# Batch 1's statistics ahead of filters and matrices, raw matrices through two buffers, three buffers for the split's second terms

## The chip, the cores and the metric

The kernel runs on one core of a Trainium2 chip. The core has five engines that matter here: PE (TensorE, matmuls and transposes), DVE (VectorE), ACT (ScalarE), POOL (GpSimd) and SP (SyncE, which here only issues transfers). Each works through its own list of instructions, in the order in which they stand there, and waits on semaphores for the others. Data lies in HBM (DRAM), in SBUF (128 partitions) and, for PE's results, in PSUM. Transfers (DMAs) are issued by SP, ACT or POOL and carried out by 16 DMA engines.

The metric is the device time of one execution in microseconds (us). The kernel before took 2992.23 us, the median of three runs (2992.15, 2992.23, 2994.43).

## The reference, cut to what matters

Input is x of shape (2, 128, 64, 64): two batches of 128 channels and 4096 positions, here called tokens. Two layers follow each other.

```python
# layer 0: group norm, four attention heads of 32 channels with rotary positions, projection, residual
xn  = groupnorm(x) * gn_w + gn_b
q, k, v = split(w_qkv @ xn + b_qkv);  q, k = rotary(q), rotary(k)
a   = softmax(q.k) v                      # 4096 x 4096 scores per batch and head
x   = xn + w_proj @ a + b_proj
# layer 1: self-attention of the normalised tokens, then a spectral layer
t   = tokens(x)
y   = layernorm(t);   t = t + softmax(y y^T) y
u   = layernorm(t)
for i, frac in enumerate((1, 2, 4, 8)):   # four branches, sequences of 4096 / frac
    s_i = sum over 16 filters k of conv(phi_k, u) @ (sigma_k ** 0.25 * Mphi[i, k]) + short convolution with Mu[i]
t   = t + sum over i of weight_i * s_i    # weight: a straight-through argmax of four numbers
```

What is spoken of below: the values v of layer 0 and the stacks of its q and k; the statistics (mean and variance of each token) of layer 1's first layernorm; and the 16 pairs of 128 x 128 matrices M_phi_plus and M_phi_minus, of each of which the weighted sum over the four branches is needed.

## The kernel before

**Layer 0** (`layer0`, lines 175 to 451) runs four units: batch 0 and batch 1, in each two pairs of heads. A unit's q and k lie in SBUF as float16 stacks `qs` and `ks` (high and low parts of the numbers above each other), its values as three bfloat16 parts. `prepare` (L207) makes them. For i in 0..7 (512 tokens each), PE projects into a PSUM tile of tag "st" (two slots of three banks), `rotate` (L228) applies the rotary tables `tab` on DVE (two L236, a sum L240, high part L241, low part L242, largest value L243), and every second i `stacks` (L275) copies the terms by 16 DMAs into `qs` and `ks`. `split` (L264) takes the values out of PSUM into the tile `left` (L268) and cuts off three bfloat16 parts: a cast (L271), and a subtraction (L273) after the first two. `table(i + 2)` loads the table after next and is kept in program order on SP.

For the first unit all of this lies ahead of or between the first scores. There, and only there (`first`), the casts L271 and L241 go to ACT, the subtractions L273 to POOL, and the DMAs of the k stacks to SP, those of the q stacks to POOL. The later units are prepared beside the attention of the unit before, where `beside` is advanced by a step at certain groups. In attention, three blocks of scores are computed by PE (L190, into the same two slots of tag "st"), exponentiated by ACT (L433) and multiplied with v (L190). All of layer 0's matmuls are kept in program order.

**Layer 1's attention** is `attend` (L876), first for batch 0, then for batch 1. It walks over 36 pairs (j, i) with j <= i of 512 x 512 blocks: the scores are symmetric, so each block serves twice. Per pair: `scores` twice (L890 on PE, L899 on ACT), `turn` four times where i > j (transposes L906, ACT L908, DVE L909), `sums` of the pair before (DVE L947 and L948 four times each, products L916, DVE L954 or L956). At i = 7 `close(j)` finishes 512 tokens (L927 to L938).

Beside it runs a chain of helpers, given as `beside`. `attend` advances it by one step (from one `yield` to the next) after each of the two `scores`, and once inside and once after `sums`. For batch 0 the chain is built at L1083 and L1084:

```python
steps = normalise(1, p1, stage, gate)
attend(0, p1, chain(left, filters(p, fw), matrices(p), steps), closed, ready)
```

- `left`: what layer 0 still has to do, the last `divide` and `project`.
- `filters` (L792): phi through two small transforms into `tables` in DRAM, 5 steps; two tiles `tb` of tag "raw".
- `matrices` (L846): the branch weights, the weighted sum `mu`, then for each k of 16 a load of 512 KB in two DMAs into `raw` (L865, L866), a step, the weighted sum on DVE (L716 and three L718), sum and difference into the same tile (L871, L872), the store to `mx` in DRAM (L873), a step. The tag "raw" has one buffer.
- `normalise(1, ...)` (L742): first the statistics of batch 1's tokens, in eight steps of four tiles (bn_stats L690, aggregate L693, then L88 on DVE and the power L89 on POOL), then eight tiles i: normalised values y (L709), high part `hi`, transposes `yT` (L757), `hiT`, and the low parts. Tile i is held back by `gate` until `close(i)` has been done, because it overwrites what batch 0's attention reads.

`ready` (L1066) loads the low parts `low` for batch 0, eight loads of 512 KB into the one buffer of tag "low", in the pairs with j = 0.

**What sets the order.** A planner of the framework turns the program into a list for each engine. Among the instructions that its own clock holds to be ready, it takes the one that stands first in the program, so an instruction can be listed far from its place when others wait longer than the planner thinks or when its buffer comes free late. Tiles of one tag get their slots in program order. `tc.keep_in_program_order` ties an instruction behind the one that stands directly before it in the program on the same engine; the first bn_stats of every four and every L709 are tied so. On the chip the lists are fixed: an engine waits at the head of its list, whatever stands behind.

Of the kernel before, what the change touches and what calls it, by code (L numbers as in the profile page):

```python
# [12 lines left out]
F32 = mybir.dt.float32  # L13
# [9 lines left out]
P = 128  # L23
B, C, HH, WW = 2, 128, 64, 64
L = HH * WW
NH = 4
CH = C // NH
# [7 lines left out]
NK = 16  # L35
NU = 3
NBR = 4
# [26 lines left out]
def conv_attn_hybrid(ctx: ExitStack, tc: tile.TileContext, io):  # L64
    nc = tc.nc
# [32 lines left out]
    def chain(*parts):  # L98
        for p in parts:
            yield from p  # L100
# [74 lines left out]
    def layer0(tok, px, last, side, beside_last):  # L175
# [3 lines left out]
        with ExitStack() as l0:  # L179
            p1 = pool(l0, "l0_1")  # L180
            p2 = pool(l0, "l0_2", 2)
# [25 lines left out]
            def prepare(b, pr, xn):  # L207
# [3 lines left out]
                u = f"{b}_{pr}"  # L211
                qs = p2.tile([P, 2, L], F16, tag="qs", name=f"qs{u}")
                ks = p2.tile([P, 2, L], F16, tag="ks", name=f"ks{u}")
# [3 lines left out]
                first = (b, pr) == (0, 0)  # L217
# [46 lines left out]
                def split(at, n, pv):  # L264

                    bvb = bv[:, 2 * CH * pr : 2 * CH * pr + 2 * CH].rearrange("p (g c) -> p g c", g=2)
                    left = p2.tile([P, n, 2, CH], F32, tag="left", name=f"left{u}_{at}", bufs=1)
                    nc.vector.tensor_tensor(left, pv, bvb.unsqueeze(1).to_broadcast([P, n, 2, CH]), ALU.add)  # L268
                    for k in range(NV):
                        dst = v[:, at : at + n, :, CH * k : CH * k + CH]  # L270
                        (nc.scalar.copy if first else nc.vector.tensor_copy)(dst, left)  # L271
                        if k + 1 < NV:
                            (nc.gpsimd if first else nc.vector).tensor_tensor(left, left, dst, ALU.subtract)  # L273

                def stacks(i2, term):  # L275
                    for s, stack in enumerate((qs, ks)):
                        for g in range(2):
                            for r in range(4):
                                src = term[r // 2 if s else r % 2]
                                at = 64 * s + CH * g  # L280
                                (nc.sync if first and s else nc.gpsimd).dma_start(
                                    stack[CH * r : CH * r + CH, g, bass.ts(i2, 1024)],
                                    src[at : at + CH, :],
                                )
# [46 lines left out]
            ao = {}  # L331
# [40 lines left out]
            qs, ks, v, steps = prepare(0, 0, xn)  # L372
# [29 lines left out]
            for n, (b, pr) in enumerate(units):  # L402
# [12 lines left out]
                for g in range(2):  # L415
                    for i in range(NQ):
                        acc = psum.tile([P, 512], F32, tag="acc", name=f"acc{b}_{pr}_{g}_{i}", bufs=1)
                        for m, tiles in enumerate(groups):
# [12 lines left out]
                            e = p2.tile([P, GT, 512], F16, tag="e", name=f"e{b}_{pr}_{g}_{i}_{m}", bufs=3)  # L431
# [10 lines left out]
                if n + 1 < len(units):  # L442
                    for _ in beside:
                        pass
                    qs, ks, v, _ = after
# [278 lines left out]
    def layers(st, layer0):  # L724
# [3 lines left out]
        tok = [tokens[b].tile([P, NI, C], F32, tag="t", name=f"tok{b}") for b in range(B)]  # L728
        px = pool(st, "px", side="right")
        right0, right1 = (st.enter_context(ExitStack()) for _ in range(2))  # L730
        last = pool(right0, "last", 2, side="right")
# [7 lines left out]
            hiT.append(px.tile([P, L], F32R, tag="a", name="hiT"))  # L739
            hi.append(Columns([px.tile([P, HALF], F32R, tag=f"b{n}", name=f"hi{n}") for n in range(2)]))  # L740

        def normalise(b, p, stage, gate=None):  # L742

            stats = LayerStats(p, tok[b], f"a{b}")
            yield from stats.steps()
            for i in range(NQ):
                while gate is not None and gate[0] <= i:
                    yield
                cols = bass.ts(i, 512)
                y = stage(i, 0)  # L750
                for t in range(4):
                    stats.normed(y[:, bass.ts(t, P)], 4 * i + t)
                nc.vector.tensor_copy(hi[0][:, cols], y)
                yield
                pt = side[0](f"yT{b}_{i}")
                for t in range(4):
                    nc.tensor.transpose(pt[:, bass.ts(t, P)], y[:, bass.ts(t, P)], ident)  # L757
                nc.vector.tensor_copy(hiT[0][:, cols], pt)
                low = (stage(i, 1), stage(i, 0)) if b == 0 else (loT[0][:, cols], lo[0][:, cols])
                for n, (src, first) in enumerate(((pt, hiT[0][:, cols]), (y, hi[0][:, cols]))):  # L760
                    nc.vector.tensor_tensor(low[n], src, first, ALU.subtract)
                    if b == 0:
                        nc.sync.dma_start(lows[i, n], low[n])
                yield

        def beside_last(stage):
            first_parts()
            stages = [stage(n) for n in range(2)]
            yield from normalise(0, last, lambda i, n: stages[n][:, i])


        left = layer0(tok, px, last, side, beside_last)
# [73 lines left out]
        def matrices(p):  # L846
            wbr = branch_weights(p)
            mu_raw = p.tile([P, NBR, NU, C], F32, tag="raw", name="mu_raw")
            nc.scalar.dma_start(mu_raw, io["mu"].rearrange("i n d e -> d i n e"))
            weighted_sum(mu, mu_raw, wbr)  # L850
            nc.sync.dma_start(gw, io["gw"])
            nc.vector.tensor_tensor(gw, gw, mask.unsqueeze(1).to_broadcast([P, 2, P]), ALU.mult)

            sig = p.tile([P, NK], F32, name="sig")
            nc.gpsimd.dma_start(sig, io["sigma"].partition_broadcast(P))
            quarter = p.tile([P, NK], F32, name="quarter")
            nc.gpsimd.memset(quarter, 0.25)
            nc.gpsimd.tensor_tensor(sig, sig, quarter, ALU.pow)
            coef = p.tile([P, NK, NBR], F32, name="coef")
            for k in range(NK):  # L860
                nc.vector.tensor_scalar(coef[:, k, :], wbr, sig[:, k : k + 1], None, ALU.mult)
            yield
            for k in range(NK):
                raw = p.tile([P, NBR, 2, C], F32, tag="raw", name=f"raw{k}")
                nc.sync.dma_start(raw[:, :, 0, :], io["mpp"][:, k].rearrange("i d e -> d i e"))  # L865
                nc.sync.dma_start(raw[:, :, 1, :], io["mpm"][:, k].rearrange("i d e -> d i e"))  # L866
                yield
                pm = p.tile([P, 2, C], F32, tag="pm", name=f"pm{k}")
                weighted_sum(pm, raw, coef[:, k, :])
                own = raw[:, 0]  # L870
                nc.vector.tensor_tensor(own[:, 0, :], pm[:, 0, :], pm[:, 1, :], ALU.add)  # L871
                nc.vector.tensor_tensor(own[:, 1, :], pm[:, 0, :], pm[:, 1, :], ALU.subtract)  # L872
                nc.sync.dma_start(mx[k], own)  # L873
                yield

        def attend(b, p, beside, closed, ready=lambda i: None):  # L876
# [181 lines left out]
        with ExitStack() as l1:  # L1058
            p1 = pool(l1, "l1")
            lo.append(p1.tile([P, L], F32R, name="lo"))  # L1060
            fw = transform(p1)
            with ExitStack() as part:
                p = pool(part, "l1_a")
                gate = [0]

                def ready(i):  # L1066
                    for n in range(2) if i == 0 else [i + 1]:
                        if n < NQ:
                            low = p.tile([P, 2, 512], F32, tag="low", name=f"low{n}")
                            nc.sync.dma_start(low, lows[n].rearrange("n p c -> p n c"))  # L1070
                            nc.vector.tensor_copy(loT[0][:, bass.ts(n, 512)], low[:, 0])
                            nc.vector.tensor_copy(lo[0][:, bass.ts(n, 512)], low[:, 1])

                def closed(j):
                    gate[0] = j + 1

                y = [None]

                def stage(i, n):
                    y[0] = p.tile([P, 512], F32, tag="y", name=f"y1_{i}")  # L1080
                    return y[0]

                steps = normalise(1, p1, stage, gate)  # L1083
                attend(0, p1, chain(left, filters(p, fw), matrices(p), steps), closed, ready)  # L1084
            right0.close()

            mxr, mxl = (x[0].rearrange("p (k s c) -> p k s c", k=NK, s=2) for x in (hiT, loT))
            with ExitStack() as part:
                p = pool(part, "l1_b", 2)
                fed = LayerStats(ffw, tok[1], "f1")  # L1090

                def closed(j):
                    fed.take(range(4 * j, 4 * j + 4))
                    fed.close(range(4 * j, 4 * j + 4))
                    own = slice(2 * j, 2 * j + 2)
                    m = p.tile([P, 2, 2, C], F32, tag="m", name=f"m{j}")
                    nc.sync.dma_start(m, mx[own].rearrange("k p s c -> p k s c"))
                    nc.vector.tensor_copy(mxr[:, own], m)
                    nc.vector.tensor_tensor(mxl[:, own], m, mxr[:, own], ALU.subtract)

                attend(1, p1, feed(0, p, bank, fw), closed)
# [321 lines left out]
```

## Time and profile before

| | |
|---|---|
| profiled execution | 2991.11 us, span 2989.3 us, clock 0.983 |
| median of three runs | 2992.23 us |
| PE busy | 2862.9 us, 96% of the span |
| DVE, ACT, POOL busy | 1738.8, 1835.8, 665.1 us |
| layer 0 | to about 1030 us; its first unit is complete at about 74 us |
| layer 1's attention, batch 0 and batch 1 | about 1030 to 1450 and 1450 to 1830 us |
| spectral layer | about 1830 to 2989 us |

The span is the time from the first to the last instruction in the trace of one execution; the device time lies a little above it. "Busy" of an engine is the time in which it executes an instruction. In the row of 40 slices each digit is the busy share of a fortieth of the span, 74.7 us. In the tables of stretches each engine's busy time is followed by its number of instructions; the columns behind are PE's granted clock as a share of the full one, the mean share of time in which a DMA engine is busy, and GB/s. In the timelines a line is the start, the duration, the engine, the line of the kernel, the operation and its tiles; in brackets stands how long the engine was idle before and what released it. SPq is the issuing of a DMA by SP.

### The profile page before, as it was taken

Reading aid. Unit: us, or ns where it says so; the run is one execution under the profiler, and the core shown is the slowest. Engines: PE = TensorE matmul, PEld = TensorE weight load, DVE = VectorE, ACT = ScalarE, POOL = GpSimd, SP = SyncE. Lnnn points to the kernel's source line nnn. Section 1 sums busy time; section 2 is a strip of 40 time slices with the busy share of each in tenths; the row PEclk is TensorE's granted clock in tenths of the full one; section 3 lists DMA queues with packets and bytes.
Section 4 is the critical chain, followed back from the end, with each engine's and each line's share of the span. In section 5 each row is a group of like instructions: output and inputs, shape, how many; then the busy total and the mean of one; then the engine's idle time right before and its main releaser. Section 6 shows DMA issues by size and latency. Waiting matters only on the chain. (4 is left out here: it accounts for less than half of the span.)

```text
span 2989.3 us, 40111 instructions
## 1 busy us (share of the span) xinstructions
PE 2862.9 (96%) x13872; PEld 1822.1 (61%) x13872; DVE 1738.8 (58%) x3060; ACT 1835.8 (61%) x2363; POOL 665.1 (22%) x1328
## 2 busy tenths in 40 slices
PE   5999999999999999399999999999999999999997
PEld 2555555555455578288677786666666666666665
DVE  5364662364252389578866777555555555556553
ACT  4999999999999844144444454444444444444542
POOL 4031130021000000100101102433444444444440
PEclk9999999999999999699999999999999999999999
DMA  5021120021010132200011001333343334333331
GB/s 147 26 82 48 54 70 4 20 71 38 5 43 24 39 99 65 62 1 1 15 36 44 12 22 50 91 96 100 83 87 84 83 79 114 80 84 82 81 83 49
DMA packets 165777, 175.91 MB, mean 59 GB/s; under 512 B 45264, under 2 KB 109536, under 8 KB 165568
## 3 DMA queue, kind: packets, MB, share of 16 engines
q1 hardware_dynamic: 121760, 136.00, 16.4%
q0 software_dynamic: 40816, 34.04, 5.4%
q10 hardware_dynamic: 2992, 3.22, 0.3%
q8 instruction: 115, 1.88, 0.3%
q14 instruction: 94, 0.77, 0.1%
HBM read 130.68 MB, written 25.49 MB: 52 GB/s over the span
## 5 line engine op out<-in xcount | busy, mean ns | idle before, releaser
L433 ACT ACTIVATE e<-s 128x1536 f16<-128x1536 f32 (+1 forms) x704 | 936.7, 1428 | 35.9 <-PE s L190 31.0
L1174 DVE TENSOR_TENSOR xl<-cv,xh 128x1024 fp32r<-128x1024 f32 x512 | 603.0, 1219 | 436.5 <-ACT xh L1173 350.0
L1173 ACT CAST xh<-cv 128x1024 fp32r<-128x1024 f32 x512 | 494.7, 1018 | 523.6 <-PE cv L1164 511.8
L1139 POOL DMA_DIRECT2D tokens_in<-rows x1024 | 490.5, 487 | 680.5 <-PE cv L1164 577.1
L190 PE MATMUL s<-qs,ks 128*128 128x512 f16 x2048 | 557.5, 379 | 8.5 <-ACT e L433 3.4
L190 PE MATMUL acc<-e,v 128*97 128x512 f16 x2048 | 557.3, 379 | 3.4 <-DVE accs L389 0.2
L1196 PE MATMUL m<-xh,loT 128*128 128x512 f32 x1024 | 409.8, 400 | 0.0
L1196 PE MATMUL m<-xh,hiT 128*128 128x512 f32 x1024 | 403.2, 394 | 0.0
L190 PEld LDWEIGHTS <-v 128*97 128x97 bf16 x2048 | 254.6, 124 | 214.5 <-issue 12.5
L899 ACT ACTIVATE ey<-y,nshift 128x512 f32<-128x512 f32 x288 | 196.1, 690 | 302.1 <-PE y L890 214.8
L190 PEld LDWEIGHTS <-ks 128*128 128x128 f16 x2048 | 200.5, 99 | 227.6 <-issue 42.3
L1164 PE MATMUL cv<-tables_in,tokens_in 32*128 32x512 f32 x2048 | 300.0, 645 | 1.4 <-DVE xl L1174 1.2
L1196 PE MATMUL m<-xl,hiT 128*128 128x512 f32 x1024 | 292.3, 417 | 1.2 <-DVE xl L1174 0.5
L1196 PEld LDWEIGHTS m<-xl,hiT 128*128 128x128 f32 x1024 | 178.8, 189 | 175.8 <-issue 104.7
L1196 PEld LDWEIGHTS m<-xh,loT 128*128 128x128 f32 x1024 | 192.7, 188 | 90.7 <-issue 47.8
L1196 PEld LDWEIGHTS m<-xh,hiT 128*128 128x128 f32 x1024 | 192.4, 188 | 42.2
L916 PE MATMUL oacc<-ep,hi 128*128 128x512 f32 x576 | 209.4, 410 | 2.7 <-DVE ep L948 1.8
L909 DVE TENSOR_TENSOR eT<-eT,eT 128x512 fp32r<-128x512 f32 x224 | 146.0, 684 | 109.4 <-ACT eT L908 108.9
L389 DVE COPY accs<-acc 97x512 f32<-97x512 f32 x64 | 44.2, 690 | 275.2 <-PE acc L190 275.1
L948 DVE TENSOR_TENSOR ep<-ey,ep 128x512 fp32r<-128x512 f32 x288 | 191.9, 683 | 5.4 <-PE oacc L916 0.4
L908 ACT ACTIVATE eT<-eT 128x512 fp32r<-128x512 f32 x224 | 133.0, 607 | 94.6 <-PE eT L906 93.9
L916 PE MATMUL oacc<-eT,hi 128*128 128x512 f32 x448 | 155.7, 409 | 3.3 <-DVE oT L956 2.3
(191 smaller groups left out, 3024.0 us busy)
## 6 DMA issues: line engine op xcount, KB each, us to landing
tables_in<-tables SPq DMA_DIRECT2D x1024, 64.0 KB, 3.4
tab<-in_rot SPq DMA_DIRECT2D x32, 512.0 KB, 4.1
tokens_in<-rows POOLq DMA_DIRECT2D x1024, 16.0 KB, 3.2
qs<-term POOLq DMA_DIRECT2D x128, 64.0 KB, 2.2
rows<-uh SPq DMA_DIRECT2D x64, 128.0 KB, 1.9
ks<-term POOLq DMA_DIRECT2D x96, 64.0 KB, 1.9
accs<-back SPq DMA_DIRECT2D x32, 128.0 KB, 2.3
lows<-stage SPq DMA_DIRECT2D x16, 256.0 KB, 2.0
```

The lines of the kernel that those rows point to most:

```text
L190: tc.keep_in_program_order(nc.tensor.matmul(*args, **kw))
L433: nc.scalar.activation(e[:, own, :], ps[:, own, :], AF.Exp, scale=SCORE_SCALE)
L899: nc.scalar.activation(e[:, 2 * h + q, :], ps[:, q, :], AF.Exp, bias=nshift, accum_out=den[:, t, i : i + 1])
L908: nc.scalar.activation(eT[0], pt, AF.Copy, accum_out=den[:, 4 * i + u, j : j + 1])
L909: nc.vector.tensor_tensor(eT[1], pt, eT[0], ALU.subtract)
L916: nc.tensor.matmul(acc, a[0][:, own], c, start=(start and t == 0 and n == 0), stop=(stop and t == len(es) - 1 and n == 2),)
L948: nc.vector.tensor_tensor(es[t][1], e[:, t, :], es[t][0], ALU.subtract)
L1139: nc.gpsimd.dma_start(ut[part, :, :], rows[b][ci, row : row + BP, w0 : w0 + WC // 2, :])
L1164: nc.tensor.matmul(pu[:, h, :], ut[grp, w % 2, :], tt[grp, w % 2, :], start=True, stop=True)
L1173: nc.scalar.copy(hi, pu.rearrange("d h (c k) -> d k h c", k=NK))
L1174: nc.vector.tensor_tensor(seconds[n % 2][:, :, w, 64 * g2 : 64 * g2 + 64].rearrange("d k (h c) -> d k h c", h=2), pu.rearrange("d h (c k) ...
L1196: nc.tensor.matmul(acc, m, x, start=(s == 0 and w == 0 and i == 0), stop=(s == 1 and w == WC - 1 and i == len(products) - 1),)
```

## The change

Four things are changed.

1. In the first unit `left` takes one of three tiles in turn, of the tags "ao0" to "ao2", which hold layer 0's attention output later on. In the other units it keeps its own tag.
2. `stacks` issues the k stack before the q stack. In the first unit, half of the q stack's DMAs (r >= 2) goes to SP instead of POOL.
3. `normalise` gets its statistics handed in. For batch 1 they are computed right after `left`, before filters and matrices; the tiles follow after the matrices as before. For batch 0 the order stays.
4. `matrices` loads k = 0 and k = 1 ahead, then k + 2 one step after matrix k has been stored. Even k use the buffer of tag "raw", odd k that of tag "low", which is of the same size.

```diff
                 def split(at, n, pv):
-                    left = p2.tile([P, n, 2, CH], F32, tag="left", name=f"left{u}_{at}", bufs=1)
+                    pool_, tag = (p1, f"ao{at // n % 3}") if first else (p2, "left")
+                    left = pool_.tile([P, n, 2, CH], F32, tag=tag, name=f"left{u}_{at}", bufs=1)
...
                 def stacks(i2, term):
-                    for s, stack in enumerate((qs, ks)):
+                    for s, stack in ((1, ks), (0, qs)):
...
-                                (nc.sync if first and s else nc.gpsimd).dma_start(
+                                (nc.sync if first and (s or r >= 2) else nc.gpsimd).dma_start(
...
-        def normalise(b, p, stage, gate=None):
-            stats = LayerStats(p, tok[b], f"a{b}")
-            yield from stats.steps()
+        def normalise(b, stats, stage, gate=None):
             for i in range(NQ):
...
-            yield from normalise(0, last, lambda i, n: stages[n][:, i])
+            stats = LayerStats(last, tok[0], "a0")
+            yield from stats.steps()
+            yield from normalise(0, stats, lambda i, n: stages[n][:, i])
...
+            raws = {}
+            def load(k):
+                if k < NK:
+                    raws[k] = p.tile([P, NBR, 2, C], F32, tag="low" if k % 2 else "raw", name=f"raw{k}")
+                    nc.sync.dma_start(raws[k][:, :, 0, :], io["mpp"][:, k].rearrange("i d e -> d i e"))
+                    nc.sync.dma_start(raws[k][:, :, 1, :], io["mpm"][:, k].rearrange("i d e -> d i e"))
+            load(0)
+            load(1)
+            yield
             for k in range(NK):
-                raw = p.tile([P, NBR, 2, C], F32, tag="raw", name=f"raw{k}")
-                nc.sync.dma_start(raw[:, :, 0, :], io["mpp"][:, k].rearrange("i d e -> d i e"))
-                nc.sync.dma_start(raw[:, :, 1, :], io["mpm"][:, k].rearrange("i d e -> d i e"))
-                yield
+                raw = raws[k]
                 pm = p.tile([P, 2, C], F32, tag="pm", name=f"pm{k}")
                 weighted_sum(pm, raw, coef[:, k, :])
...
                 nc.sync.dma_start(mx[k], own)
+                yield
+                load(k + 2)
                 yield
...
-                steps = normalise(1, p1, stage, gate)
-                attend(0, p1, chain(left, filters(p, fw), matrices(p), steps), closed, ready)
+                stats = LayerStats(p1, tok[1], "a1")
+                steps = chain(left, stats.steps(), filters(p, fw), matrices(p), normalise(1, stats, stage, gate))
+                attend(0, p1, steps, closed, ready)
```

## The prediction

> **What bounds the kernel now.** I read the page first: TensorE works 96% of the span, so only time in which it stands can be won.
>
> ```profile
> span 2989.3 us, 40111 instructions
> PE   5999999999999999399999999999999999999997
> PEclk9999999999999999699999999999999999999999
> ```
>
> Three of 40 slices show it idle: the first, the seventeenth (1196 to 1270 us) and the last. The change touches the first two. The busy time by stretch measures the second and its surroundings (columns: length, PE, weight loads, DVE, ACT, POOL, clock, DMA):
>
> ```profile
> 1040.00:1208.00 168.00, 166.38 (x816) 133.49 (x814) 150.97 (x336) 81.22 (x247) 0.59 (x1) 0.99 0.27 82
> 1208.00:1268.80 60.80, 11.78 (x40) 8.31 (x41) 31.11 (x127) 3.66 (x11) 8.29 (x9) 0.52 0.21 62
> 1270.00:1310.00 40.00, 40.00 (x204) 32.52 (x203) 29.08 (x56) 20.01 (x62) 0.00 (x0) 1.00 0.00 1
> 1440.00:1470.00 30.00, 25.29 (x110) 17.72 (x109) 29.91 (x123) 15.17 (x44) 8.09 (x8) 0.93 0.00 1
> ```
>
> PE is full before and after; in 60.8 us between it does 28 transposes and 11 products, at half clock. At full clock these take 28 x 0.1 (eight in 0.79 us at 1047.67) + 11 x 0.23 = 5.3 us: the hole costs 55.5. The timeline says why:
>
> ```profile
> 1210.36 0.35 DVE L716 TENSOR_SCALAR pm<-raw,coef 128x256 f32<-128x256 f32 x1 [2.03 <-DMA raw<-in_mpm]
> ...
> 1212.83 0.34 SPq L873 DMA_DIRECT2D mx<-raw  x1
> 1214.56 0.37 SPq L865 DMA_DIRECT2D raw<-in_mpp  x1
> 1214.97 0.51 SPq L866 DMA_DIRECT2D raw<-in_mpm  x1
> 1218.44 0.35 DVE L716 TENSOR_SCALAR pm<-raw,coef 128x256 f32<-128x256 f32 x1 [5.63 <-DMA raw<-in_mpm]
> ...
> 1245.01 0.28 DVE L872 TENSOR_TENSOR raw<-pm 128x128 f32<-128x128 f32 x1
> 1245.21 0.48 DVE L690 BATCH_NORM_STATS2 lsta<-tok 128x6 f32<-128x128 f32 x2
> ...
> 1248.42 0.45 PE L757 MATMUL yT<-ident,y 128*128 128x128 f32 x1 [40.45 <-DVE lmva L693]
> ```
>
> Five matrices (k = 11 to 15) run with no attention between them, one per 8.1 us: 2.4 of arithmetic, a store (1.7), a load (3.9) into the only buffer. Then come the statistics, and PE's next instruction is a transpose of what they normalise.
>
> In the first unit, the timelines of POOL, DVE, PE and SP:
>
> ```profile
> 34.23 3.43 POOL L281 DMA_DIRECT2D qs<-term  x7 [0.16 <-issue]
> 37.68 0.67 POOL L273 TENSOR_TENSOR left<-left,v 128x256 f32<-128x256 f32 x1
> 41.06 0.42 DVE L268 TENSOR_TENSOR left<-first,bv 128x256 f32<-128x256 f32 x1
> 41.62 2.04 PE L190 MATMUL first<-xn,wqk 128*128 128x512 f32 x2 [6.72 <-DVE left L268]
> 73.53 1.44 PE L190 MATMUL s<-qs,ks 128*128 128x512 f16 x3 [2.98 <-DMA ks<-term]
> 33.24 5.06 SPq L281 DMA_DIRECT2D ks<-term  x8
> ```
>
> The third split writes the one `left` only at 41.06, after POOL's subtraction, queued behind eight issues of q stacks; PE waited 6.72 us for the PSUM tile that this frees. The stage ends at 73.53, when the last k stack lands and the ninth group of scores starts.
>
> **What the Trainium skill says.** "TensorE: Matmul & The Clock Gate", "Architectural detail": PE's queue pulls only weight loads ahead, DVE's is strict first in, first out. The trace agrees: matmuls stood 40.45 us behind one transpose, DVE stood in front of each load. Same page, "What's actually happening": an idle window of about 3.4 us halves the clock; here 0.52 in the hole. "DMA: Bandwidth & Descriptors", "Rules for kernel authors": issue a load early, wait late. Before, a load waits for its predecessor's store (1.7 us), so it can't be early. Same page, "Issuing engines are not separate DMA queues": another issuer saves only issue time; here 0.63 us each on SP, 0.49 on POOL.
>
> **Statistics ahead.** Attention over batch 0 calls the helper chain at four places per pair (j, i): pair n takes step 4n-1 after its first scores, 4n after its second, 4n+1 inside the sums of pair n-1 and 4n+2 after them; pair 0 takes steps 1 and 2. The chain owes 11 steps of layer 0's last `divide` and `project` (7 + 4), 5 of filters, 33 of matrices. So the last matrix, k = 15, is computed at step 49 and the first statistics at step 50, and between these two lies only PE work: the first bn_stats, kept in program order, is pinned directly behind L872. The normalised tile follows at step 59, its transpose at 60, in pair 15. But the raw buffer lets the planner place only one matrix per pair (10 us) where the steps ask for two, so at pair 15 five matrices were still to do, and the pin made all wait for them. After: statistics at steps 12 to 19 (pairs 3 to 5), each behind a DVE instruction of attention or an earlier statistic; filters 21 to 25; matrices 26 to 59; first L709 at 60, transpose at 61. Between steps 58 (k = 15) and 60 lie turns of pair 14, so this L709 is pinned behind an L909, not behind L872. Batch 1's tokens are complete at 1064.5 and pair 3 runs around 1066: the statistics wait for nothing new. They carry no DMA, and their 8 POOL powers of 1.0 us are needed a hundred us later: nothing. So the hole goes: -55.5.
>
> Filters and matrices move back by nine steps, 23 us, with their DMAs (phi's consumers, two table stores, the loads of mu, gw and ends, 16 x 3 for matrices, all behind the low loads in SP's queue). The stored matrices are first used on DVE at 1526.9, the tables loaded from 1744: nothing, with 300 us of cover.
>
> **Two buffers.** The odd matrices use the tag of the low loads, free at 1089.5, before raw0's issue at 1096.8 (now nearer 1120): no wait for memory. Each buffer still turns in about 8.1 us, so matrices come every 4.05, two per pair of 10.2. In SP's queue load k+2 waits for store k (1.7) and holds store k+1 behind it: 0.34 + 1.4 + 0.88 = 2.6 per matrix of 4.05, no bound. DMA share rises from 0.23 to about 0.46 there, so loads may take longer than 3.9. Between attention's instructions the arithmetic of one matrix is spread over 4.0 us (1100.79 to 1104.86) instead of 2.4, which leaves about 0.6 of a pair's 10.2 to spare: waits of a few us in all can remain, and they stand inside the sum for DVE that follows.
>
> **What comes back.** DVE worked in the hole, and this now stands beside attention: the same stretch, first for the tile raw, then for the statistics' tile:
>
> ```profile
> 1208.00:1268.80 60.80, 11.50 (x30) 0.52 0.21 62
> 1208.00:1268.80 60.80, 10.59 (x64) 0.52 0.21 62
> ```
>
> Together 22.1 us. From 1040 to 1208 DVE has 168 - 151.0 = 17.0 idle: 5.1 too little. A full DVE doesn't keep PE full: from 1440 to 1470, with another set of statistics in attention, DVE is busy 29.91 of 30 and PE loses 4.7. So +5.1 + 4.7, about +10. The normalised tiles 0 and 1 (two of 3.4) fall into stretches where DVE idles 10.9 of 40: nothing. Bounds: +4 if only the shortage counts, +25 if DVE lags through all of pairs 3 to 17 (15 pairs at the 1.6 us per 10 of 1440 to 1470).
>
> **First unit.** With three `left` buffers, in tiles not used before 100 us, DVE can run rotations 3.8 us apart (26.42, 30.22, 34.03): eight end at 56.8, not 69.7: -12.9 at most. SP now carries 12 stack issues per two tiles instead of 8: 12 x 0.63 + 2 x 0.65 for the tables pinned behind them = 8.9 against DVE's 7.6. So the fourth stacks start at 33.2 + 3 x 8.9 = 59.9 and the keys can be used 3.8 later, 63.7: -9.8. The PSUM slots hold more back: scores and the last projections alternate in two, exponentials at best 2.4 apart (59.23, 61.63). Walked through: the q rows of the first scores are ninth and tenth on SP, so these start at 34 + 6.3 + 2 = 42.3; the fifth table is issued behind twelve stacks at 41.6 and lands at 46, its rotation frees the second scores' slot at 48; two projections (3.1 each), three scores (2.0), the last projection and three scores end at 64; its terms are ready at 64.2, four issues (2.5) and the landing (2) give 68.7: -5. POOL's 4 issues fewer (2.0 us) lie inside this. k first is worth nothing more: the scores need both. Bounds: -12.9, and +5 if nothing is won and two table pairs each come four issues (2.5) late.
>
> **Sum.** 2989.3 - 55.5 + 10 - 5 = 2938.8 span. The profiled run took 2991.11, 1.8 over its span, and the median is 1.1 above it: 2941.7.
>
> **Rivals.** (1) DVE becomes the bound: +25, and the first unit wins nothing: 2992.2 - 55.5 + 25 = 2962. For it: DVE at 90% before 1208. Against: PE was full there with DVE at 9.7 to 9.9 of 10 from 1050 to 1070. The same region covers a stall that survives at half length (five matrices at 4.05, 20 us). (2) All goes well: -55.5 + 4 - 10 = 2931. (3) Slower: the planner takes the two-buffer loads as landed early and puts matrices on DVE in one block without attention, as it did with five. Sixteen at 4.05 are 65 us; from fourteen on (14 x 4.05 = 56.7) the block costs more than the hole; with the first unit's worst +5, 2992.2 - 55.5 + 65 + 5 = 3007. Against: nothing waits for the matrices any more, attention's DVE work is ready between them. (4) The change doesn't do what it says: another pin takes the place of this one, the hole stays, and only the first unit's -5 counts: 2987, within what a measurement can't tell.
>
> **How the numbers follow.** My forecast 0.60 (own range 2931 to 2953), rival 1 0.20, rival 2 0.12, rival 3 0.05, rival 4 0.03. The range 2929 to 2964 leaves out rivals 3 and 4 and the tails. Measurement tells 0.2%, 6 us, from no change: faster 0.93, same 0.02, slower 0.05.
>
> **What would show it.** Right: no slice of PE under 9 near 1200; statistics L690 between 1060 and 1090; L716 two per pair with waits under 1 us; DVE at 95% or more from 1060 to 1200; first `ks` wait before 70; no 6.72 wait. Wrong: a PE wait above 10 us on y or on ep, a block of L716 without L947, or SP's table loads holding L236.

## The result, and the profile after

| | before | after |
|---|---|---|
| median of four runs | 2992.19 us (2988.70 to 2994.43) | 2941.02 us (2939.38 to 2941.48) |
| profiled execution, span | 2991.11, 2989.3 us | 2940.61, 2938.4 us |

The ratio of the times is 0.9829 with a 95% interval of 0.9812 to 0.9846: 51 us less. The prediction's sum was 2941.7, its range 2929 to 2964.

First the page of the kernel after: its span and the two rows of 40 slices (73.5 us each) for PE and its clock.

```profile
span 2938.4 us, 40073 instructions
PE   5999999999999999999999999999999999999997
PEclk9999999999999999999999999999999999999999
```

The 3 in the seventeenth slice is gone, and the clock's 6 with it. Next, PE's waits between 1020 and 1250 us (line waited for and its releaser: us in total, times, longest); before, the head of such a list from 1020 to 1270 was `yT`, waiting 47.9 us in 2 waits.

```profile
PE y L903 <- DVE loT L1084: 5.1, 1, 5.1
PE eT L919 <- DVE eT L922: 2.2, 4, 0.9
PE y L903 <- ACT ey L912: 2.0, 2, 1.0
PE eT L919 <- DVE loT L762: 1.6, 1, 1.6
PE oacc L929 <- DVE ep L961: 1.6, 4, 0.9
```

The 5.1 us stand at the start of attention, where before lost 5.5 in the same way. All others are short. By stretch (columns as ahead of the prediction: length, PE, weight loads, DVE, ACT, POOL, clock, DMA share, GB/s):

```profile
1040.00:1100.00 60.00, 60.00 (x302) 47.72 (x301) 58.49 (x181) 29.43 (x88) 10.61 (x9) 1.00 0.25 82
...
1120.00:1220.00 100.00, 91.85 (x445) 70.18 (x444) 96.21 (x233) 44.94 (x134) 0.10 (x1) 1.00 0.34 100
...
1230.00:1260.00 30.00, 30.00 (x151) 24.46 (x150) 21.61 (x42) 14.74 (x48) 0.00 (x0) 1.00 0.00 1
...
1390.00:1430.00 40.00, 35.26 (x161) 25.09 (x160) 39.60 (x146) 17.59 (x50) 8.11 (x8) 1.00 0.05 15
```

Batch 1's statistics now run from 1063.1 to 1082.1 (L692). In the first line, which holds them, DVE is at 97% and PE does not stand at all: they cost nothing. The loss is in the second line. From 1119.2 to 1200.1 the sixteen matrices are computed, and PE stands 8.15 of 100 us, 6.4 of them up to 1200. The last line is the passage to batch 1's attention: 4.7 us, as before in its 1440 to 1470.

Between markers that both traces have, the time divides so:

| stretch | before | after | difference | predicted |
|---|---|---|---|---|
| first rotation (L236) to the end of the first unit (first copy of `accs`) | 55.1 | 50.9 | -4.2 | -5 |
| attention from its first product (`oacc`) to `close(1)` (its `fin`) | 154.5 | 164.5 | +10.0 | +10 |
| `close(1)` to the last product of batch 1 | 635.9 | 577.9 | -58.0 | -55.5 |
| from there to the end, the spectral part above all | 1157.8 | 1158.5 | +0.7 | 0 |

The stretches that the table leaves out differ by +0.8 and -0.2. Eight matmuls of scores and four transposes that PE did behind the marker `close(1)` before are done ahead of it after. At the prediction's 0.23 and 0.1 us they are 2.2 us, an estimate, so the hole itself is nearer to -55.8 and the loss nearer to +7.8.

In the first unit, DVE, PE and SP of the kernel after (timeline: start, duration, engine, line, operation, in brackets the idle time before and its releaser):

```profile
36.74 1.10 PE L190 MATMUL first<-xn,wqk 128*128 128x512 f32 x2 [1.02 <-DVE left L270]
41.78 1.30 SPq L224 DMA_DIRECT2D tab<-in_rot  x2
46.80 1.41 DVE L236 SCALAR_TENSOR_TENSOR t<-first,bqk,tab 128x512 f32<-128x512 f32 x2 [4.09 <-DMA tab<-in_rot]
47.01 1.44 PE L190 MATMUL s<-qs,ks 128*128 128x512 f16 x3 [4.30 <-ACT e L435]
71.81 0.81 PE L190 MATMUL s<-qs,ks 128*128 128x512 f16 x3 [2.44 <-DMA ks<-term]
```

The wait of 6.72 us for `left` has shrunk to 1.02. In its place DVE waits 4.09 us for a table that SP issued at 41.78, behind the stacks, and PE's second group of scores 4.30 for exponentials. The ninth group of scores starts at 71.81, 44.6 us after the first rotation instead of 47.1.

### The profile page after: what moved, and what is told of

The parts are those of the page before. It is cut to its first block, busy times and chain, and to the rows that moved or that the text cites. A ratio compares the mean times of both kernels' runs of the same rounds, so it can differ in the third digit from the quotient of the medians.

```text
span 2938.4 us, 40073 instructions
## 1 busy us (share of the span) xinstructions
PE 2856.3 (97%) x13872; PEld 1814.5 (62%) x13872; DVE 1734.4 (59%) x3060; ACT 1837.7 (63%) x2363; POOL 660.3 (22%) x1312
## 5 line engine op out<-in xcount | busy, mean ns | idle before, releaser
L1188 DVE TENSOR_TENSOR xl<-cv,xh 128x1024 fp32r<-128x1024 f32 x512 | 603.3, 1220 | 435.3 <-ACT xh L1187 347.9
L912 ACT ACTIVATE ey<-y,nshift 128x512 f32<-128x512 f32 x288 | 195.9, 690 | 284.3 <-PE y L903 184.0
L922 DVE TENSOR_TENSOR eT<-eT,eT 128x512 fp32r<-128x512 f32 x224 | 147.2, 685 | 99.1 <-ACT eT L921 98.4
L961 DVE TENSOR_TENSOR ep<-ey,ep 128x512 fp32r<-128x512 f32 x288 | 192.0, 684 | 4.3 <-PE oacc L929 0.4
```

Of the source, the lines that this page charges most:

```text
L912: nc.scalar.activation(e[:, 2 * h + q, :], ps[:, q, :], AF.Exp, bias=nshift, accum_out=den[:, t, i : i + 1])
L922: nc.vector.tensor_tensor(eT[1], pt, eT[0], ALU.subtract)
L961: nc.vector.tensor_tensor(es[t][1], e[:, t, :], es[t][0], ALU.subtract)
L1188: nc.vector.tensor_tensor(seconds[n % 2][:, :, w, 64 * g2 : 64 * g2 + 64].rearrange("d k (h c) -> d k h c", h=2), pu.rearrange("d h (c k) ...
```

## The experiments

Four questions were put: is it really the pin behind the last matrix that made the hole; what is each of the three parts worth alone; where do the 10 us come from that are lost again; and can they be had back? Each ratio below is to the kernel before, measured beside it on the same chip. Its medians there were 2990.71 us beside the empty step, the statistics alone, the two buffers alone and the first unit alone; 2991.72 beside the kernel after, one buffer, the slower pace and the third table; and 2990.45 beside the other four.

**One empty step behind the matrices.** If the pinned first bn_stats stands behind L872 only because no DVE work lies between the two steps, one more step must free it, with one buffer and the statistics where they were.

```diff
                 nc.sync.dma_start(mx[k], own)
                 yield
+            yield
```

> The kernel before with one empty step after the last matrix, nothing else. Theory A (the pin: the first bn_stats is tied directly behind the last matrix's L872, since no DVE instruction stands between the two steps): one more step puts an L909 of attention between them, the statistics are tied behind that one, and the hole of 55 us goes although the raw buffer stays single: 2935 to 2955 us. Theory B (the single raw buffer, 8 us per matrix, is what attention waits for): nothing changes, 2985 to 2995 us. Theory C (both parts are needed): at most half, 2960 to 2980 us.

Measured: 2948.23 us (2947.11 to 2950.26), ratio 0.9857 [0.9842, 0.9873]. The waits of its PE from 1035 to 1460:

```profile
PE y L891 <- DVE loT L1072: 5.6, 1, 5.6
PE oacc L917 <- DVE ep L949: 3.7, 8, 1.3
PE oacc L917 <- DVE ep L948: 2.3, 4, 1.3
```

The wait of 40 us is gone, though the buffer is single and nothing was moved ahead. On DVE the first statistics now follow a subtraction of attention, as theory A has it (its L909 is L910 here):

```profile
1167.36 1.29 DVE L910 TENSOR_TENSOR eT<-eT,eT 128x512 fp32r<-128x512 f32 x2 [1.21 <-ACT eT L909]
1168.56 0.48 DVE L690 BATCH_NORM_STATS2 lsta<-tok 128x6 f32<-128x128 f32 x2
```

The last matrix is computed only at 1253. So the pin is shown to be the cause, and the five late matrices alone were not: they are spread over pairs here, since nothing holds attention behind them. The statistics now fall on the matrices, at 1168 and later, and PE loses 6.6 us from 1160 to 1220.

**The statistics ahead, alone.** Parts 1, 2 and 4 of the change are left out.

```diff
...
-                steps = normalise(1, p1, stage, gate)
-                attend(0, p1, chain(left, filters(p, fw), matrices(p), steps), closed, ready)
+                stats = LayerStats(p1, tok[1], "a1")
+                steps = chain(left, stats.steps(), filters(p, fw), matrices(p), normalise(1, stats, stage, gate))
+                attend(0, p1, steps, closed, ready)
```

> The kernel before with the statistics of batch 1 ahead of filters and matrices alone; one raw buffer, first unit as before. Theory A: the hole goes, matrices come one per pair as the one buffer allows, so DVE is less crowded than in the changed kernel: 2935 to 2948 us. Theory B: matrices still hold up attention, the hole stays for the most part: 2970 to 2992 us.

Measured: 2939.82 us (2937.73 to 2942.79), 0.9828 [0.9813, 0.9843]. This part alone gives as much as the whole change, without the first unit's gain, as theory A expected. The other parts together must then bring nothing, though one of them is a gain.

**The two buffers, alone.**

```diff
...
+            load(0)
+            load(1)
+            yield
             for k in range(NK):
-                raw = p.tile([P, NBR, 2, C], F32, tag="raw", name=f"raw{k}")
...
+                raw = raws[k]
...
                 nc.sync.dma_start(mx[k], own)
+                yield
+                load(k + 2)
                 yield
```

> The kernel before with two raw buffers alone; statistics stay behind the matrices. Theory A: the tie stays, but at two matrices per pair all sixteen are done by the time of the statistics' step, so the hole goes here too, less what crowding on DVE takes: 2940 to 2955 us. Theory B: the hole goes, 2940 to 2955 us as well. Theory C: at most half goes, 2960 to 2980 us. What tells A from B is the pair of this run and the two others.

Measured: 2961.38 us (2960.06 to 2965.31), 0.9905 [0.989, 0.992]. It breaks the pin too (it adds a step), but gives only 29 us. The number is the one that theory C expected, but the trace shows another reason than that both parts are needed. SP's issues and one of PE's waits in its trace:

```profile
1060.33 0.36 SPq L1080 DMA_DIRECT2D low<-lows  x1
1064.78 0.37 SPq L868 DMA_DIRECT2D raw<-in_mpp  x1
...
1111.49 0.37 SPq L1080 DMA_DIRECT2D low<-lows  x1
...
1126.55 0.37 SPq L1080 DMA_DIRECT2D low<-lows  x1
```

```profile
PE y L900 <- DVE loT L1081: 8.8, 1, 8.8
```

The odd matrices share the buffer of the low loads. Without the statistics' steps ahead of them, the load of matrix 1 is written in the program before low tile 6, and matrix 3 before low tile 7. The slots go in program order, so these two low tiles wait for a matrix to be computed and stored, and PE stands 8.8 us for the scores that need them. In the whole change all eight low tiles come first: there the statistics keep this collision away.

**The two buffers with a buffer of their own.** As above, but odd matrices in a tile of tag "ao3", which is free then.

```diff
-                    raws[k] = p.tile([P, NBR, 2, C], F32, tag="low" if k % 2 else "raw", name=f"raw{k}")
+                    pool_, tag = (last, "ao3") if k % 2 else (p, "raw")
+                    raws[k] = pool_.tile([P, NBR, 2, C], F32, tag=tag, name=f"raw{k}", bufs=1)
```

> The kernel with two raw buffers alone (statistics behind the matrices), but the odd matrices in a buffer of their own (tag ao3, free by then) instead of the low loads' buffer. In the run before, raw1 was issued at 1064.8 ahead of the last two low loads, which then waited for matrices until 1111.5 and 1126.6, and PE stood 8.8 us and more for a low part. If that is why two buffers alone won only 29 us: 2940 to 2951 us. If the tie behind the matrices is why: 2957 to 2965 us.

Measured: 2949.37 us (2947.01 to 2952.81), 0.9867 [0.9852, 0.9882]. The shared buffer had cost 12 us. What is left, -41.1 us, is the gain of the empty step (-42.5) and no more: all in all the second buffer brings nothing. In the traces a loss and a gain cancel: up to `close(1)` it takes 169.5 us against 164.6 with the empty step, from there to the last product 576.3 against 583.0.

**The first unit, alone, and the three `left` buffers, alone.** The first kernel has parts 1 and 2 of the change, the second only this:

```diff
-                    left = p2.tile([P, n, 2, CH], F32, tag="left", name=f"left{u}_{at}", bufs=1)
+                    pool_, tag = (p1, f"ao{at // n % 3}") if first else (p2, "left")
+                    left = pool_.tile([P, n, 2, CH], F32, tag=tag, name=f"left{u}_{at}", bufs=1)
```

> The kernel before with the first unit's edits alone (three left buffers, k first, half of the q stack's DMAs on SP). By the traces of before and after the first copy of an accumulator came 3.5 us earlier (81.6 to 78.1) and the last one of layer 0 2.7: 2988 to 2990 us, against 2987 of the prediction's -5. If the first unit's gain is lost to another order of the lists later on, 2992 us.

> The kernel before with the three left buffers of the first unit alone; stacks as before. If the one left buffer was the first unit's whole loss (PE waited 6.7 us for it) and the new order of the stacks adds nothing: as much as the whole first-unit edit, 2983 to 2987 us. If the queue of q stacks on POOL in front of the subtraction was the loss: less than half of it, 2988 to 2991 us.

Measured: both parts 2983.93 us (2981.32 to 2988.29), 0.9978 [0.9971, 0.9985]; `left` alone 2984.27 us (2982.84 to 2986.65), 0.9978 [0.997, 0.9987]. So -6.8 and -6.2 us: more than the 4 us of the trace and more than was expected of the first kernel. The buffers alone explain it; the order and the queues of the stacks add nothing that can be told. In the trace of `left` alone the ninth scores come even earlier:

```profile
69.21 1.44 PE L190 MATMUL s<-qs,ks 128*128 128x512 f16 x3 [3.02 <-DMA ks<-term]
```

That is 41.3 us after its first rotation (at 27.89), against 44.8 with the stacks reordered; the unit ends 49.4 us after it, against 51.1. DVE does not wait for a table in it. These are single traces, and the unit varies from one to the next: it takes 54.9 to 58.7 us in the five kernels that have it as before, and 50.5 to 53.0 in the seven that have parts 1 and 2 and nothing else in it.

**The kernel after again, and with one raw buffer.** The second kernel keeps parts 1 to 3 and has the matrices as before.

```diff
...
-            load(0)
-            load(1)
-            yield
             for k in range(NK):
-                raw = raws[k]
+                raw = p.tile([P, NBR, 2, C], F32, tag="raw", name=f"raw{k}")
...
-                yield
-                load(k + 2)
                 yield
```

> The changed kernel itself beside the next three, on the same chip: 2939 to 2943 us.

> The changed kernel with matrices as before: one raw buffer, loaded one step ahead. Theory D (the second buffer crowds DVE: two matrices of 1.85 us per pair instead of one, where DVE has 3 us idle, and PE loses 8 us between 1120 and 1220): faster than the changed kernel by 4 to 8 us, 2932 to 2937 us. Theory E (the parts add up, the second buffer gains or costs nothing once the statistics are ahead): the same as the changed kernel within 3 us, 2938 to 2944 us. Theory F (the second buffer is needed): slower, over 2950 us.

Measured: after 2943.02 us (2937.86 to 2946.64), 0.9836 [0.9823, 0.985]; one buffer 2930.43 us (2929.41 to 2932.38), 0.9798 [0.9785, 0.9812]. Leaving the second buffer out makes the kernel 12.6 us faster, more than the 4 to 8 of theory D; E and F are out. The stretch from the first product to `close(1)` takes 155.1 us instead of 166.6. The next kernel asks whether it is the buffer or the pace.

**Two buffers at a slower pace.** The kernel after with two more empty steps per matrix.

```diff
                 load(k + 2)
                 yield
+                yield
+                yield
```

> The changed kernel with two more empty steps per matrix: both buffers, but one matrix per pair. Theory D: the same gain as with one buffer, 2932 to 2937 us, since it is DVE's crowding by the pace and not the buffer. If what costs in the changed kernel is the transfers (waits for raw, 3.5 us in all) or batch 1's statistics alone: 2938 to 2943 us.

Measured: 2930.26 us (2929.4 to 2935.09), 0.9797 [0.9783, 0.981]: the same as one buffer, and again a little under theory D's range. In its trace a matrix comes every 7.2 us, 1.4 per pair and not one, against 5.1 in the trace after. So it is the pace that costs, and not the second buffer as such. The stretch 1120 to 1220 of the two, one buffer first:

```profile
1120.00:1220.00 100.00, 97.64 (x493) 78.00 (x492) 93.36 (x210) 49.32 (x149) 0.00 (x0) 1.00 0.22 66
```

```profile
1120.00:1220.00 100.00, 99.59 (x498) 80.33 (x498) 96.89 (x224) 49.33 (x148) 0.00 (x0) 1.00 0.31 90
```

The amount of transfers is no rival: 90 GB/s here with PE full, 100 after. The reader should not stop at DVE's busy share: it is 96.89 here with PE full and was 96.21 after with PE short of 8 us. What differs is what DVE had to get done in the time. One matrix, interleaved with attention, in the trace after:

```profile
1149.86 0.35 DVE L718 TENSOR_SCALAR pm<-raw,coef 128x256 f32<-128x256 f32 x1
1150.12 0.42 DVE L960 CAST ep<-ey 128x512 fp32r<-128x512 f32 x1
1150.46 0.48 DVE L720 SCALAR_TENSOR_TENSOR pm<-raw,coef,pm 128x256 f32<-128x256 f32 x1
1150.86 0.68 DVE L967 TENSOR_TENSOR oT<-oacc,oT 128x512 f32<-128x512 f32 x1
1151.46 0.48 DVE L720 SCALAR_TENSOR_TENSOR pm<-raw,coef,pm 128x256 f32<-128x256 f32 x1
1151.85 0.69 DVE L961 TENSOR_TENSOR ep<-ey,ep 128x512 fp32r<-128x512 f32 x1
1152.45 0.48 DVE L720 SCALAR_TENSOR_TENSOR pm<-raw,coef,pm 128x256 f32<-128x256 f32 x1
1152.85 0.42 DVE L960 CAST ep<-ey 128x512 fp32r<-128x512 f32 x1
1153.18 0.29 DVE L882 TENSOR_TENSOR raw<-pm 128x128 f32<-128x128 f32 x1
1153.39 0.28 DVE L883 TENSOR_TENSOR raw<-pm 128x128 f32<-128x128 f32 x1
1153.59 0.69 DVE L922 TENSOR_TENSOR eT<-eT,eT 128x512 fp32r<-128x512 f32 x1
```

From start to start, DVE spends 0.26 + 3 x 0.40 + 0.21 + 0.20 = 1.87 us on it. Attention alone takes DVE 21.61 of 30 us (1230 to 1260, above), 7.3 of a pair's 10.2. Two matrices per pair make 7.3 + 3.7 = 11.0: 0.8 too much, 6.4 us over eight pairs, and the waits for raw matrices in this stretch (2.9 us) bring it to 9.3; this is an estimate. Measured: 8.15 us of PE in the window, 7.8 to 10.0 by the markers, 12.6 between the two kernels. Over the time that the sixteen matrices took, DVE's load is 0.72 + 16 x 1.87 / length: 1.09 after (80.9 us long), 0.99 at the slower pace (111), 0.92 with one buffer (153). Of these three only the first exceeds one, and only it loses. The planner also orders DVE's list otherwise in each of them, so that DVE is crowded by the pace is argued from this sum and not shown apart.

**A third table in the first unit.** Added to the kernel with one buffer: every third table goes into a tile of its own, so that SP can issue it before the stacks.

```diff
-                        tab = p2.tile([P, 2, 512], F32, tag="tab", name=f"tab{u}_{i}")
+                        if first and i % 3 == 2:
+                            tab = last.tile([P, 2, 512], F32, tag="ao3", name=f"tab{u}_{i}", bufs=1)
+                        else:
+                            tab = p2.tile([P, 2, 512], F32, tag="tab", name=f"tab{u}_{i}")
...
-                    table(i + 2)
+                    table(i + 3 if first else i + 2)
...
-                    for i in range(2):
+                    for i in range(3 if first else 2):
                         table(i)
```

> The kernel with one raw buffer again, and a third buffer for the rotary tables of the first unit (tag ao3, free until then), so that each table is issued one rotation earlier, ahead of the stacks. If the first unit lost part of its gain because the tables are queued behind twelve stack issues (DVE waited 4.1 and 2.2 us for them in the changed kernel): 2 to 5 us less than the kernel with one buffer. If PSUM slots and exponentials set the first unit's end: the same within 2 us.

Measured: 2931.34 us (2930.74 to 2934.45), 0.9801 [0.9788, 0.9815]: no gain. In its trace DVE no longer waits for a table (7.8 us in 2 waits with one buffer), but all the longer for PE's projection (11.4 us in 4 waits, against 4.4 in 3), and the first unit takes 52.1 us. The wait has only moved: PE did not give DVE the next tile earlier.

**The sums on POOL, with two buffers and with one.** If DVE's load is the cause, taking L882 and L883 off it should bring the loss back: 0.41 us per matrix, 0.8 per pair, just the shortage.

```diff
-                nc.vector.tensor_tensor(own[:, 0, :], pm[:, 0, :], pm[:, 1, :], ALU.add)
-                nc.vector.tensor_tensor(own[:, 1, :], pm[:, 0, :], pm[:, 1, :], ALU.subtract)
+                nc.gpsimd.tensor_tensor(own[:, 0, :], pm[:, 0, :], pm[:, 1, :], ALU.add)
+                nc.gpsimd.tensor_tensor(own[:, 1, :], pm[:, 0, :], pm[:, 1, :], ALU.subtract)
```

> The changed kernel with the last sum and difference of each matrix (L882, L883) on POOL, which takes 0.4 of 1.85 us per matrix from DVE and keeps everything else. Theory D (crowding: two matrices in each of some eight pairs are 3.7 us beside 6.9 of attention, 10.6 in 10.2): the load falls to 9.8 per pair, under the pair's length, and half or more of the 9 to 12 us comes back: 2931 to 2938 us. If the loss comes from transfers or from the order of PE's list: 2939 to 2944 us.

> The kernel with one raw buffer, statistics ahead and the first unit's edits, with the sum and difference on POOL as well. Theory D: at one matrix per pair DVE is below its pair's length anyway, so the relief is worth little: 2926 to 2931 us. If relief of DVE counts everywhere: as much as in the changed kernel, 2921 to 2926 us.

Measured: with two buffers 2943.17 us (2940.11 to 2944.2), 0.984 [0.9827, 0.9854], as the kernel after; with one 2947.95 us (2947.04 to 2950.95), 0.9858 [0.9843, 0.9873], 17.5 us slower than with the sums on DVE. Theory D missed both. The first result lies in the range given for transfers or the order of PE's list, the second in no range. The traces tell more. With two buffers, the stretch 1120 to 1220, DVE's waits in it, and two of POOL's sums:

```profile
1120.00:1220.00 100.00, 91.63 (x437) 69.69 (x435) 88.52 (x198) 44.19 (x131) 22.17 (x33) 0.98 0.33 100
```

```profile
DVE pm L718 <- DMA raw<-in_mpm: 7.8, 6, 2.0
DVE pm L718 <- POOL raw L883: 2.5, 5, 0.8
```

```profile
1154.02 0.46 POOL L882 TENSOR_TENSOR raw<-pm 128x128 f32<-128x128 f32 x1 [3.24 <-issue]
...
1159.99 2.07 POOL L882 TENSOR_TENSOR raw<-pm 128x128 f32<-128x128 f32 x1 [5.09 <-DVE pm L720]
```

DVE is relieved of 7.7 us (96.21 to 88.52; 16 x 0.41 is 6.6), and waits 10.3 us for raw matrices where it waited 2.9: 7.4 more. What was taken from its work came back as waiting at the head of its list, and PE stands as long as before (8.4 us). So this run can't tell DVE's crowding from these waits. A matrix is stored later when POOL finishes it, the buffer comes free later, and L718 of a later matrix stands in DVE's list in front of attention's work. With one buffer most matrices show it (1110 to 1300):

```profile
DVE pm L718 <- DMA raw<-in_mpm: 19.7, 13, 3.5
```

against 3.2 us in 4 waits with the sums on DVE. From 1120 to 1300 its PE is busy 164.9 us instead of 177.5. The load doesn't explain this: with the waits it comes to 0.99 (0.72 + 16 x 1.46 / 161.8 + 19.7 / 161.8), and the slower pace loses nothing at that. The waits themselves do, as its longest shows:

```profile
1257.20 0.35 DVE L718 TENSOR_SCALAR pm<-raw,coef 128x256 f32<-128x256 f32 x1 [3.48 <-DMA raw<-in_mpm]
...
1259.03 1.28 DVE L912 TENSOR_TENSOR eT<-eT,eT 128x512 fp32r<-128x512 f32 x2
...
1259.77 1.25 PE L909 MATMUL eT<-ident,ey 128*128 128x128 f32 x8 [2.89 <-DVE eT L912]
```

ACT had delivered the operand of attention's L912 by 1255.8, but L912 stood in DVE's list behind the matrix, and PE's transposes waited for L912. Of the ten waits for a raw matrix longer than 1 us, nine are followed within 5.2 us by such a stand of PE, 13.8 us together. In the kernel after, only 1.8 of PE's 7.1 us in stands over 0.3 follow such a wait. What stays open is where the waits come from. From the end of a matrix's weighted sum to the end of its second sum it is 1.4 us (median) with POOL and 1.0 with DVE; but the planner also ordered DVE's list otherwise, and neither was tried alone.

## Why the prediction was right, and where it was not

**The hole.** Right in cause and size: -58.0 for -55.5, about -55.8 without the instructions that changed sides of the marker. The pin behind L872 was its cause, as the empty step shows; "the statistics wait for nothing new" and cost PE nothing.

**What comes back.** The size was right, +10.0 by the markers (about +7.8 without those instructions) for +10, but by luck: the account was wrong. The prediction set 22.1 us of DVE's work against 17.0 idle over the whole stretch 1040 to 1208 and added 4.7 for a DVE that is full with statistics. But the statistics landed where PE did not stand for them, the 4.7 of the passage are there before and after, and the loss lies beside the matrices. The step that failed is the average over 168 us. The matrices fall into eighty of them, two per pair, and there DVE owes attention's 7.3 us plus 2 x 1.87, which exceeds a pair's 10.2 by 0.8. "Two buffers" did look at one pair, but at the turn of a buffer (load 3.9, store 1.7, arithmetic 4.0, so "about 0.6" of 10.2 to spare) and not at DVE's sum with attention. A shortage must be summed where the work falls, at its rate, not over a stretch that averages full and empty pairs. So the second buffer, which got no price of its own, costs 12.6 us beside the statistics ahead.

**Two buffers' other steps.** "Two per pair" held (sixteen in 80.9 us, 5.1 apart), and so did "no wait for memory" in the whole change; of DVE's waits for raw two were longer than the 1 us that was named (1.4 and 1.0). These waits fell from 26.1 us to 3.5, but with one buffer and the statistics ahead they are 3.2: the fall comes from taking away the pin and not from the second buffer. Once the pin is gone nobody waits for the matrices, so an earlier load was worth nothing. The rule of the Trainium skill that the prediction cited ("DMA: Bandwidth & Descriptors", "Rules for kernel authors") is about overlapping a transfer with compute; one buffer did that already.

**First unit.** The walk held to the microsecond in its first half: the first scores at 41.90 (42.3 in the walk), the fifth table issued at 41.78 (41.6), its rotation over at 48.2 (48). But the second scores started at 47.01, before that rotation was over, released by exponentials; the walk had tied them to the rotation. The ninth scores came at 71.81, not 68.7, and the unit gained 4.2 us in the trace for the predicted 5; the runs say 6 to 7. That the gain is the `left` buffers' was right: alone they are worth as much. That the q stacks on SP limit it is not borne out by the times, though the ninth scores come 3.5 us later with them (44.8 against 41.3 after the first rotation). The sign "no 6.72 wait" was right, "first `ks` wait before 70" wrong.

**Rivals.** (1), DVE becomes the bound at +25, was right in kind, for sixteen matrices instead of fifteen pairs of lag, and wrong in size. (2), all goes well at 2931, is what the kernel reaches without its second buffer, 2930.4; the agreement is chance, since the loss that it leaves out is the second buffer's. (3), a block of matrices without attention, didn't come; (4), another pin, neither.

## What to carry to other kernels

When an engine stands long behind one instruction, look for what that instruction is tied to in the list: here one empty step gave 42 us, and faster loads gave nothing more. Before helper work is sped up, add it to what the shared engine already does per turn of the main loop; if the sum exceeds the turn, a slower pace is the better one, and a second buffer is a loss. That sum is not enough: an instruction that waits for a transfer holds up all that stands behind it in its engine's list, even where the engine has time. So moving work to an idle engine gains only if nothing waits longer for its result; and test parts one by one, since a right total can hide a gain and a loss of the same size.

## What the runs showed of the hardware

POOL's sum of 128x128 took 0.45 to 0.54 us in 44 of the 64 cases of the two kernels, and 0.71 to 2.66 in the other 20. Each of these 20 ran beside a cast of DVE or a subtraction with both operands in SBUF (L960 and L961 with two buffers), such as those from 1159.78 to 1161.74 beside the 2.07 above, and it took the longer the longer it did: 0.79 us with 0.47 beside them, 2.66 with 2.35. Beside DVE's subtractions and sums that read PSUM (L922, L967) it kept its 0.46. DVE's own durations hardly moved (L720 478 ns before and 481 after the sums were moved, L961 685 and 694). This agrees with the Trainium skill, "SBUF — State Buffer", "SBUF: two separate sides", by which VectorE and GpSimd share a pair of ports that one of them holds for a whole instruction while the other is blocked, if VectorE's instruction is in a mode that uses both pairs or has two inputs in SBUF. No run was made to test it apart.
